# A four-layer graph network on one core: new order of work and a buffer of its own for h ahead of the attention layers

## The chip, the cores and the metric

One core of a Trainium2 chip runs the whole program. The metric is the device time of one execution in microseconds; several runs of a kernel are given by their median. A profile is one such execution, recorded instruction by instruction.

## What is computed

The reference has 3327 nodes with 256 features and a sparse adjacency matrix `adj` (3327 x 3327, int32, about 0.5% ones). Layer 0:

```
h = x @ Wt.T + bt                          # 3327 x 64
s = leaky_relu(h @ Wa.T + ba, 0.2)         # one score per node
scores = where(adj > 0, s, -9e15)
neighbor = softmax(scores, axis=1) @ h
x = layer_norm(x + neighbor @ Wp.T + bp) * gamma + beta
```

The score belongs to the row, so within a row all neighbours have one weight and all others another. Row i of `neighbor` follows from the number of its neighbours, the sum of h over them, and the sum of h over all nodes.

Layers 1 to 3 are attention over the same graph with 8 heads of 32, and a feed-forward part of width 1024:

```
q, k, v = split(layer_norm(x) @ w_qkv)
attn = softmax(where(adj != 0, q @ k.T * 32**-0.5, -inf))
x = x + (attn @ v) @ w_proj + b_proj
x = x + gelu(layer_norm(x) @ w1 + b1) @ w2 + b2
```

## The kernel before, in words

Nodes lie in 26 blocks of 128 rows (`NB`; the last has 127), blocks in 7 groups of four (the last has two). The kernel writes the order of instructions of every engine by hand: each engine runs its instructions in the order in which the Python code issues them, and waits where an operand or a buffer is not ready. So a call's place in the code is its place in five queues at once. TensorE is PE in the profile, VectorE DVE, ScalarE ACT, GpSimd POOL and SyncE SP.

Layer 0 does two things with `adj` at once: it computes the layer, and it makes for each node a list of up to 40 neighbours (`LMAX`), because layers 1 to 3 gather the k and v rows of listed neighbours only. Per block i, `Block` (L694) has these steps:

- `load` (L700): SyncE loads 128 rows of `adj` as int32 into one of three buffers with the tag `a32`.
- `sign` (L707): ScalarE turns them into 0 and 1 in bf16 (`abf`, three buffers); VectorE (blocks 0 to 2) or GpSimd clears the padding column.
- `turn` (L716): TensorE transposes the 26 tiles of 128 x 128, ScalarE copies them to `aT`.
- `candidates` (L726): VectorE multiplies by column numbers (L731) and takes the 8 largest of each of 16 segments of 208 columns (L735).
- `list` (L737): VectorE takes the 40 largest of these 128 (L741 to L748).

For h, `x_turn` (L782) transposes a group of x, `h_of` (L793) multiplies and VectorE adds the bias (L804). `split_h` (L808) writes h as three bf16 parts side by side. `of_h` (L821) makes `S.fold` from the identity, the column sum `S.hsum` (26 fp32 matmuls, L829) and the scores `S.s`. The tile `S.h` (L777) comes from the `a32` buffers. `sums` (L850) multiplies the parts of h by the turned blocks, two blocks at a time.

Per group, `Group` (L841) has the rest of layer 0 as steps: `copy` and `back` (sums out of PSUM and turned back), `soft` (weights; L889 to L918 on VectorE, 12 to 15 small matmuls into `places`, two exponentials on ScalarE, L919), `mix` (L934; it ends by calling `place`, L923, which reads `places` and forms ranks), `project` (L953), `add` (L967, with a norm's statistics), `norm` (ScalarE, L977), `norm1` (L983), `turn1` (L993), `qkv0` and `qkv2` (L1001, two blocks each, with a store of k and v), and `store` (L1018, two stores). `project` and `turn1` and `qkv` share three PSUM banks (`bank`, L628).

The stretch from L1043 to L1079 is written out call by call: three blocks are loaded, signed and turned, the lists of blocks 0 and 1 made, then the groups of h with pieces of blocks 2 and 3 between them, then `split_h`, `sums(1)`, `of_h`, `turn(4)`, `sums(3)`, `copy` of group 0, load, sign and turn of block 5, and `sums(5)`. The loop from L1108 runs over blocks 4 to 25. Each pass loads, signs and turns block i + 2, makes candidates and list of block i, and runs the group steps of two half slots, `plan[2 * i]` ahead of the candidates and `plan[2 * i + 1]` ahead of the list. `plan` (L1083 to L1102) gives each step a half slot:

```
names = ("copy", "back", "soft", "mix", "project", "add", "norm", "norm1", "turn1",
         "qkv0", "qkv2", "store")
...
    at = dict(zip(names, (0, 1, 3, 4, 5, 6, 7, 8, 9, 10, 11, 12)))
    first = 8 * g + 4
    if g == 0:
        first = 8
        at["copy"] = -9
        at["back"] = 0
```

After the loop, nodes are sorted by number of neighbours. The sort's first part (L1128 to L1147) makes ranks, the second (L1153 to L1185) a permutation `perm` by one-hot products (`pp_perm` L1178, `pf` L1182). The last two groups' remaining steps stand around these. GpSimd then gathers the rows of the sorted blocks (`gather_rows`, L1262), loads of weights and biases follow (`load_rest`, L1242), and layers 1 to 3 run over the sorted blocks: GpSimd gathers k and v rows neighbour by neighbour (L1303, 1344 instructions over three layers), VectorE forms scores and weighted values (L1325, L1326, L1366), TensorE adds them up and does the dense parts. All of `Layer` is untouched by the change. A second path for graphs that don't fit (`general_path`) is not taken.

Of the kernel before, what the change touches and what calls it, by code (L numbers as in the profile page):

```python
# [8 lines left out]
FP = mybir.dt.float32  # L9
BF = mybir.dt.bfloat16  # L10
# [7 lines left out]
P = 128  # L18
N = 3327
# [4 lines left out]
H0 = 64  # L24
# [499 lines left out]
def sparse_path(ctx, tc, ins, out, dram, flag):  # L524
# [98 lines left out]
    with tc.tile_pool(name="a", bufs=1) as a, tc.tile_pool(name="aw", bufs=2) as aw, \  # L623
# [42 lines left out]
        nrow = 2 * D + 2 * H0 + 1  # L666
        row = a.tile([1, nrow], FP, name="s_row")
        o = 0
# [5 lines left out]

        zero = a.tile([1, KVW[1]], FP, name="zero")
        nc.vector.memset(zero, 0.0)
# [17 lines left out]
        class Block:  # L694


            def __init__(self, i):
                self.i, self.r = i, ROWS[i]

            def load(self):  # L700
                i, r = self.i, self.r
                a32 = aw.tile([P, N], I32, tag="a32", bufs=3, name=f"s_a32_{i}")
                for p0, p1 in (((0, P),) if r == P else ((0, r // 16 * 16), (r // 16 * 16, r))):
                    nc.sync.dma_start(a32[p0:p1], ins["adj"][i * P + p0:i * P + p1, :])
                self.a32 = a32

            def sign(self):  # L707
                i, r = self.i, self.r
                self.abf = aw.tile([P, PADDED], BF, tag="abf", bufs=3, name=f"s_abf_{i}")

                (nc.vector if i < 3 else nc.gpsimd).memset(self.abf[:, N:], 0.0)  # L711
                if r < P:
                    nc.gpsimd.memset(self.abf[96:P, :], 0.0)
                nc.scalar.sign(self.abf[:r, :N], self.a32[:r])  # L714

# [10 lines left out]
            def candidates(self, part=None):  # L726

                i = self.i
                if not part:
                    v = self.v = aw.tile([P, NSEG, SEG], BF, tag="v", name=f"s_v_{i}")  # L730
                    nc.vector.tensor_mul(v, self.abf.rearrange("p (s c) -> p s c", c=SEG),  # L731
                                         seg1[:, None, :].to_broadcast([P, NSEG, SEG]))
                    self.cand = aw.tile([P, NSEG, 8], FP, tag="cand", name=f"cand_{i}")
                for s in range(NSEG) if part is None else range(part * 4, part * 4 + 4):
                    nc.vector.max(out=self.cand[:, s, :], in_=self.v[:, s, :])  # L735

# [14 lines left out]
        def weights0():  # L751

            S.wtT = a.tile([P, 2, H0], FP, name="s_wtT")

            S.wpT = a.tile([H0 + 1, D], FP, name="s_wpT")
            nc.sync.dma_start(S.wpT[H0:, :], ins["L0_gnn_bp"][None, :])
            S.nT = a.tile([H0 + 1, 512], FP, name="s_nT")
            nc.vector.memset(S.nT[H0:, :], 1.0)
            pt, pt2 = bank("s_pt_w"), bank("s_pt_w2")
            for c in range(2):  # L760
                nc.tensor.transpose(pt[:, c * H0:(c + 1) * H0], wt_raw[:, c * P:(c + 1) * P],
                                    ident[:H0, :H0])
                nc.tensor.transpose(pt2[:H0, c * P:(c + 1) * P], wp_raw[:, c, :], ident)
            nc.scalar.copy(S.wtT, pt[:, :2 * H0].rearrange("p (c h) -> p c h", c=2))
            nc.scalar.copy(S.wpT[:H0], pt2[:H0, :D])
            brow = a.tile([P, nrow], FP, name="s_brow")
            for c0 in range(0, nrow, 512):
                cw = min(512, nrow - c0)
                pb = bank(f"s_pb_row_{c0}")
                nc.tensor.matmul(pb[:, :cw], ones[0:1, :], row[:, c0:c0 + cw],  # L770
                                 start=True, stop=True)
                nc.scalar.copy(brow[:, c0:c0 + cw], pb[:, :cw])
            S.gam_b, S.bet_b = (brow[:, k * D:(k + 1) * D] for k in range(2))
            S.bt_b = brow[:, 2 * D:2 * D + H0]
            S.wa_b = brow[:, 2 * D + H0:2 * D + 2 * H0]
            S.ba_b = brow[:, nrow - 1:nrow]
            S.h = aw.tile([P, NB, H0], FP, tag="a32", bufs=3, name="s_h")  # L777
            nc.vector.memset(S.h[96:P, NB - 1, :], 0.0)
# [41 lines left out]

        def of_h():  # L821

            S.fold = a.tile([P, H0], FP, name="s_fold")
            nc.vector.tensor_copy(S.fold, ident[:, :H0])
            nc.vector.tensor_add(S.fold, S.fold, ident[:, H0:])
            ph = bank("s_phsum")
# [4 lines left out]
            S.hsum = a.tile([P, H0], FP, name="s_hsum")  # L831
            nc.scalar.copy(S.hsum, ph[:, :H0])

            t = aw.tile([P, NB, H0], FP, tag="v", name="s_h_wa")
# [6 lines left out]
        class Group:  # L841
# [92 lines left out]
            def mix(self):  # L934
# [15 lines left out]
                nc.vector.tensor_add(nb, nb, t3)  # L950
                self.place()

# [95 lines left out]
        for i in range(2):  # L1048
# [6 lines left out]
        pieces = [lambda i=i, k=k: blk[i].candidates(k) if k < 4 else blk[i].list()  # L1055
                  for i in (2, 3) for k in range(5)]
        NG = len(GROUPS)
        for g in range(NG):
            x_turn(g)
            if g:  # L1060
                h_of(g - 1)
            if g == 2:
                turn(3)
            if g == 4:
                blk[4].load()
                blk[4].sign()
            for _ in range(2 if g > 3 else 1):
                pieces.pop(0)()
        h_of(NG - 1)
        split_h()  # L1070
        sums(1)
        of_h()
        turn(4)
        sums(3)
        groups[0].copy()
        blk[5].load()
        blk[5].sign()
        turn(5)
        sums(5)  # L1079

        names = ("copy", "back", "soft", "mix", "project", "add", "norm", "norm1", "turn1",  # L1083
                 "qkv0", "qkv2", "store")
        plan = [[] for _ in range(2 * NB)]
        for g in reversed(range(NG)):
            at = dict(zip(names, (0, 1, 3, 4, 5, 6, 7, 8, 9, 10, 11, 12)))
            first = 8 * g + 4
            if g == 0:
                first = 8  # L1090
                at["copy"] = -9
                at["back"] = 0
            elif g == NG - 2:
                at.update(norm=6, norm1=7, turn1=7, qkv0=99, qkv2=99, store=99)
            elif g == NG - 1:
                first = 2 * NB - 4
                at.update(soft=2, mix=3, project=3, add=99, norm=99, norm1=99, turn1=99, qkv0=99,
                          qkv2=99, store=99)
# [9 lines left out]
        for i in range(4, NB):  # L1108
# [3 lines left out]
            for s in plan[2 * i]:  # L1112
                step(*s)
            blk[i].candidates()
            if i + 2 < NB:
# [3 lines left out]
            for s in plan[2 * i + 1]:  # L1119
                step(*s)  # L1120
            blk[i].list()
        last = groups[-2:]
        last[0].qkv(0)
        last[0].qkv(2)
# [23 lines left out]

        last[1].add()
        last[1].norm()  # L1150

# [11 lines left out]
        nc.vector.tensor_copy(num_bf, num)  # L1163
        last[1].norm1()
        last[1].turn1()
        last[1].qkv(0)
        last[1].store()
        oh_lo = aw.tile([P, NB, P], BF, tag="v", name="oh_lo")
# [471 lines left out]
```

## Time and profile before

| What | Value |
|---|---|
| Median of 3 runs | 2555.74 us (2554.16 to 2559.1) |
| Profiled execution, its own time | 2555.05 us |
| Its span, first to last instruction | 2553.3 us |
| Mean granted TensorE clock | 0.782 |
| First gather of sorted rows (L1263, GpSimd) | 498.05 us from the span's start |
| Neighbour gathers, L1303 | 1344 instructions, mean 947 ns, 1272.7 us busy |
| Rows L735, maxima of 8 | 416 instructions, mean 360 ns, 118.0 us busy |
| Row L731, products with column numbers | 26 in layer 0, mean 1883 ns |

A row of the profile names a line of the kernel, an engine, an operation, what is written and read, how many instructions there are and how long they ran. In a timeline a row has its start in the span, its length, and in brackets how long the engine sat idle before it and what ended that. The list of waits sums such idle times by the pair of waiting and releasing lines. The clock is a share of TensorE's full speed. The mean of L735 in the list of groups is that of the records; in a timeline sixteen of them take 4.52 us, since they overlap.

### The profile page before, as it was taken

How to read it: one execution, taken by the hardware profiler on the slowest of the kernel's cores; microseconds unless marked ns; L12 is line 12 of the kernel's file. 1: busy time of each engine (PE TensorE's matmuls, PEld its weight loads, DVE VectorE, ACT ScalarE, POOL GpSimd, SP SyncE). 2: the span in 40 equal slices, each digit the busy share in tenths (PEclk: the TensorE clock that was granted, in tenths of full speed). 3: DMA queues.
4: the chain of work that ended last, by engine and by line, in shares of the span. 5: the costliest groups of instructions: out<-in, count | busy, mean ns of one | idle time of the engine just before them, and what ended most of it. 6: DMA issues, size and time to landing. Idle time of an engine off the chain costs nothing.

```text
span 2553.3 us, 24048 instructions
## 1 busy us (share of the span) xinstructions
PE 1667.7 (65%) x7561; PEld 1119.4 (44%) x7561; DVE 1939.2 (76%) x3983; ACT 781.8 (31%) x1321; POOL 1361.1 (53%) x1458
## 2 busy tenths in 40 slices
PE   5668775426588787865276778777733666766667
PEld 4545553214444454544244445445422444434444
DVE  6697999568888887764788988878537868777864
ACT  5346663201243333332022233333210221222222
POOL 4000000177777776631777767656137767777671
PEclk9768777657788788887577888788865877987888
DMA  6324430377777777753777767756347756766672
GB/s 255 108 98 165 162 116 35 116 232 217 230 211 232 229 220 204 205 117 109 212 210 216 215 190 218 211 174 179 72 152 209 211 169 189 210 187 189 187 193 54
DMA packets 144487, 453.80 MB, mean 178 GB/s; under 512 B 29522, under 2 KB 40157, under 8 KB 141022
## 3 DMA queue, kind: packets, MB, share of 16 engines
q0 software_dynamic: 113056, 370.26, 51.3%
q1 hardware_dynamic: 9834, 53.90, 6.0%
q10 hardware_dynamic: 21458, 28.02, 3.1%
q8 instruction: 61, 1.00, 0.2%
q14 instruction: 78, 0.63, 0.1%
HBM read 420.64 MB, written 31.42 MB: 177 GB/s over the span
## 4 chain that ended last, share of the span: by engine, by line
PE 17%; DVE 15%; DMA 12%; POOL 9%; issue 9%; ACT 2%; DVEq 0%; ACTq 0%; POOLq 0%; SPq 0%
DMA kv<-kv,t 11%; POOL kv L1303 8%; PE pu L1440 5%; PE py L1463 4%; DVE kv L1325 4%; PE po L1372 3%; DVE vw L1366 3%; DVE sc L1326 3%; PE pk L1493 2%; PE po L1396 1%; POOL out_dram L1506 1%; DVE t L1481 1%; DVE st_n L575 1%; PE py L1456 0%; PE pq L1493 0%
## 5 line engine op out<-in xcount | busy, mean ns | idle before, releaser
L1303 POOL DMA_INDIRECT kv<-kv,t x1344 | 1272.7, 947 | 641.3 <-issue 355.7
L1372 PE MATMUL po<-s_ident,vw 128*128 128x128 f32 x2688 | 456.3, 327 | 514.0 <-DVE vw L1366 512.8
L1372 PEld LDWEIGHTS po<-s_ident,vw 128*128 128x128 f32 x2688 | 381.4, 170 | 641.5 <-DVE vw L1366 543.7
L1325 DVE TENSOR_TENSOR kv<-kv,q 128x1024 f32<-128x1024 f32 (+3 forms) x363 | 413.6, 1139 | 311.8 <-DMA kv<-kv,t 195.4
L1326 DVE TENSOR_REDUCE sc<-kv 128x32 f32<-128x1024 f32 (+3 forms) x363 | 414.1, 1141 | 12.4
L1366 DVE TENSOR_TENSOR vw<-kv,w 128x1024 f32<-128x1024 f32 x333 | 372.3, 1128 | 1.7
L1440 PE MATMUL pu<-fT,s_w 128*128 128x512 f32 (+2 forms) x768 | 322.8, 555 | 2.9 <-ACT fT L596 2.9
L1463 PE MATMUL py<-gT,s_w 128*128 128x512 f32 (+1 forms) x672 | 283.6, 550 | 0.0
L1446 ACT ACTIVATE gT<-pu,pvb 128x512 f32<-128x512 f32 (+2 forms) x192 | 116.6, 608 | 380.0 <-PE pu L1440 379.5
L1440 PEld LDWEIGHTS pu<-fT,s_w 128*128 128x128 f32 x768 | 151.8, 211 | 124.8 <-issue 91.1
L711 POOL MEMSET s_abf<- 128x1 bf16 x23 | 2.2, 105 | 356.0 <-DVE s_v L731 239.1
L1463 PEld LDWEIGHTS py<-gT,s_w 128*128 128x128 f32 x672 | 124.6, 192 | 102.9 <-issue 66.1
L735 DVE MAX8 cand<-s_v 128x8 f32<-128x208 bf16 x416 | 118.0, 360 | 0.9
L1493 PE MATMUL pk<-s_w_qkv,nT 128*128 128x512 f32 x208 | 109.6, 653 | 6.1 <-ACT nT L596 6.1
L588 ACT ACTIVATE xn_f<-t,nm_f,rqy_f 128x256 f32<-128x256 f32 x78 | 43.2, 594 | 217.7 <-DVE nm_f L582 211.0
L591 PE MATMUL pf<-s_ident,xn_f 128*128 128x128 f32 x156 | 46.0, 436 | 97.7 <-ACT xn_f L588 97.5
L723 PE MATMUL s_ptb<-s_ident_bf,s_abf 128*128 128x128 bf16 x676 | 67.0, 265 | 64.1 <-ACT s_abf L714 48.7
L1396 PE MATMUL po<-s_w_proj,oT 128*128 128x256 f32 x312 | 101.0, 455 | 0.0
L1340 ACT ACTIVATE sc<-sc,mx 128x120 f32<-128x120 f32 (+6 forms) x78 | 32.0, 410 | 204.9 <-DVE mx L1337 204.4
L723 PEld LDWEIGHTS <-s_abf 128*128 128x128 bf16 x676 | 56.6, 122 | 78.3 <-ACT s_abf L714 55.0
L724 ACT COPY s_aT<-s_ptb 128x896 bf16<-128x896 bf16 x104 | 82.3, 859 | 20.5 <-PE s_ptb L723 20.5
L855 PE MATMUL s_pa<-s_aT,s_hs 128*128 128x256 bf16 x338 | 80.0, 285 | 13.2 <-DVE s_hs L817 13.2
(290 smaller groups left out, 2176.1 us busy)
## 6 DMA issues: line engine op xcount, KB each, us to landing
s_a<-in_adj_dram SPq DMA_DIRECT2D x25, 1663.5 KB
kv<-kv,t POOLq DMA_INDIRECT x1344, 3.8
kv<-kvr ACTq DMA_DIRECT2D x52, 256.0 KB
kv<-s_kvr ACTq DMA_DIRECT2D x26, 256.0 KB
s_w<-in_L_gnn_w_dram SPq DMA_DIRECT2D x6, 1024.0 KB
t<-ql ACTq DMA_DIRECT2D x6, 592.0 KB
t<-s_x ACTq DMA_DIRECT2D x6, 512.0 KB
s_w_qkv<-in_L_gnn_w_qkv_dram SPq DMA_DIRECT2D x3, 768.0 KB
```

Source lines behind the costliest of these rows:

```text
L723: nc.tensor.transpose(pt[:, m, :], self.abf[:, k * P:(k + 1) * P], ident_bf)
L735: nc.vector.max(out=self.cand[:, s, :], in_=self.v[:, s, :])
L1303: nc.gpsimd.indirect_dma_start(out=t[:, s, :], out_offset=None, in_=kv[L], in_offset=bass.IndirectOffsetOnAxis(ap=t2[:, b, k:k + 1].bitcas ...
L1325: nc.vector.tensor_mul(k, k, self.q[b][:, None, :].to_broadcast([P, n, D]))
L1326: nc.vector.tensor_reduce(self.sc[b][:, s0:s0 + n, :], k.rearrange("p s (h d) -> p s h d", d=HD), AX.X, ALU.add)
L1366: nc.vector.tensor_mul(vw[:, :n * D].rearrange("p (s h d) -> p s h d", h=HEADS, d=HD), v, self.wp[b][:, s0:s0 + n, :, None].to_broadcast([ ...
L1372: nc.tensor.matmul(self.po[b][:, k * P:(k + 1) * P], vw[:, at:at + P], ident, is_transpose=True, start=(s0 + s == 0 and k == 0), stop=(s0 ...
L1396: nc.tensor.matmul(ps, c["oT"][:, k * P:(k + 1) * P], w["w_proj"][:, k, :], start=False, stop=(k == 1))
L1440: nc.tensor.matmul(c["pu", f][:, :n], w["w1"][:, e, f * P:(f + 1) * P], c["hT"][:, e, :n], start=(e == 0), stop=(e == 1))
L1446: nc.scalar.activation(g[:, :n], c.pop(("pu", f))[:, :n], AF.Gelu_apprx_tanh, bias=w["b1"][:, f:f + 1])
L1463: nc.tensor.matmul(c["py"][e][:, :n], w["w2"][:, f, e * P:(e + 1) * P], g[:, :n], start=(f == 0), stop=last)
L1493: nc.tensor.matmul(ps[:, :c1 - c0], c["hT"][:, e, j * P:(j + 1) * P], nxt["w_qkv"][:, e, c0:c1], start=(e == 0), stop=(e == 1))
```

## The change

The change is ahead of the layers only; five edits stand in one diff.

- h gets a buffer of its own instead of one of the three `a32` buffers. In return the one-row tiles `row` and `zero` use the buffers with the tag `ql`.
- Block 0 is loaded, signed and multiplied in two column halves (1664 and 1663), each with its own instruction.
- Between the parts of h, the candidates and the list of block 2 come in one piece ahead of h's first part; block 3 follows in five pieces, and a first piece of block 4 is added; its other pieces come after `sums(5)`.
- `S.fold` is made in `weights0`. The column sum (`sum_h`, new, the code is that of `of_h`) comes ahead of `split_h`; load and sign of block 5 come ahead of `sums(1)`; `back` of group 0 ahead of `sums(5)`; `of_h`'s remaining part comes last. The steps of group 0 from `soft` on stand half a slot later, and `place` is a step of its own, next to `project`. Block 4 has nothing to do for VectorE in the loop.
- After the loop, `add` and `norm` of the last group stand ahead of the qkv of the group before, and its `norm1`, `turn1`, `qkv` and `store` ahead of the sort's second part.

```diff
-        row = a.tile([1, nrow], FP, name="s_row")
+        row = aw.tile([1, nrow], FP, tag="ql", name="s_row")
...
-        zero = a.tile([1, KVW[1]], FP, name="zero")
+        zero = aw.tile([1, KVW[1]], FP, tag="ql", name="zero")
...
+                mid = NSEG // 2 * SEG
+                self.cols = [(0, mid), (mid, PADDED)] if i == 0 else [(0, PADDED)]
...
-                    nc.sync.dma_start(a32[p0:p1], ins["adj"][i * P + p0:i * P + p1, :])
+                    for c0, c1 in self.cols:
+                        c1 = min(c1, N)
+                        nc.sync.dma_start(a32[p0:p1, c0:c1],
+                                          ins["adj"][i * P + p0:i * P + p1, c0:c1])
...
-                nc.scalar.sign(self.abf[:r, :N], self.a32[:r])
+                for c0, c1 in self.cols:
+                    c1 = min(c1, N)
+                    nc.scalar.sign(self.abf[:r, c0:c1], self.a32[:r, c0:c1])
...
-                    v = self.v = aw.tile([P, NSEG, SEG], BF, tag="v", name=f"s_v_{i}")
-                    nc.vector.tensor_mul(v, self.abf.rearrange("p (s c) -> p s c", c=SEG),
-                                         seg1[:, None, :].to_broadcast([P, NSEG, SEG]))
+                    self.v = aw.tile([P, NSEG, SEG], BF, tag="v", name=f"s_v_{i}")
...
+                    for c0, c1 in self.cols:
+                        if s * SEG == c0:
+                            nc.vector.tensor_mul(
+                                self.v[:, s:c1 // SEG, :],
+                                self.abf[:, c0:c1].rearrange("p (s c) -> p s c", c=SEG),
+                                seg1[:, None, :].to_broadcast([P, c1 // SEG - s, SEG]))
...
-            S.h = aw.tile([P, NB, H0], FP, tag="a32", bufs=3, name="s_h")
+            S.h = a.tile([P, NB, H0], FP, name="s_h")
...
-                self.place()
...
-                  for i in (2, 3) for k in range(5)]
+                  for i in (2, 3, 4) for k in range(5)]
         NG = len(GROUPS)
         for g in range(NG):
             x_turn(g)
+            if g == 1:
+
+                for _ in range(5):
+                    pieces.pop(0)()
             if g:
                 h_of(g - 1)
+                pieces.pop(0)()
...
-            for _ in range(2 if g > 3 else 1):
-                pieces.pop(0)()
         h_of(NG - 1)
+        sum_h()
         split_h()
+        blk[5].load()
+        blk[5].sign()
         sums(1)
-        of_h()
         turn(4)
         sums(3)
         groups[0].copy()
-        blk[5].load()
-        blk[5].sign()
         turn(5)
+        groups[0].back()
         sums(5)
+        for piece in pieces:
+            piece()
+        of_h()
...
-            at = dict(zip(names, (0, 1, 3, 4, 5, 6, 7, 8, 9, 10, 11, 12)))
+            at = dict(zip(names, (0, 1, 3, 4, 5, 5, 6, 7, 8, 9, 10, 11, 12)))
             first = 8 * g + 4
             if g == 0:
                 first = 8
-                at["copy"] = -9
-                at["back"] = 0
+                at = {k: v + 1 for k, v in at.items()}
+                at["copy"] = at["back"] = -9
...
-            blk[i].candidates()
+            if i > 4:
+                blk[i].candidates()
...
-            blk[i].list()
+            if i > 4:
+                blk[i].list()
         last = groups[-2:]
+        last[1].add()
+        last[1].norm()
         last[0].qkv(0)
...
-        last[1].add()
-        last[1].norm()
+        last[1].norm1()
+        last[1].turn1()
+        last[1].qkv(0)
+        last[1].store()
...
-        last[1].norm1()
-        last[1].turn1()
-        last[1].qkv(0)
-        last[1].store()
```

More of the change, by code (lines that the diff above doesn't have):

```diff
@@ L751, in weights0 @@
         def weights0():
+            S.fold = a.tile([P, H0], FP, name="s_fold")
+            nc.vector.tensor_copy(S.fold, ident[:, :H0])
+            nc.vector.tensor_add(S.fold, S.fold, ident[:, H0:])
             S.wtT = a.tile([P, 2, H0], FP, name="s_wtT")
@@ L819, in split_h, with sum_h @@
             nc.vector.tensor_copy(hs[:, :, 2 * H0:3 * H0], rest)
[L821 to L825, printed above, removed]
+        def sum_h():
             ph = bank("s_phsum")
@@ L832, in of_h @@
             nc.scalar.copy(S.hsum, ph[:, :H0])
+        def of_h():
             t = aw.tile([P, NB, H0], FP, tag="v", name="s_h_wa")
@@ L1075, in sparse_path @@
         groups[0].copy()
-        blk[5].load()
-        blk[5].sign()
         turn(5)
+        groups[0].back()
         sums(5)
-        names = ("copy", "back", "soft", "mix", "project", "add", "norm", "norm1", "turn1",
+        for piece in pieces:
+            piece()
+        of_h()
+        names = ("copy", "back", "soft", "mix", "place", "project", "add", "norm", "norm1", "turn1",
                  "qkv0", "qkv2", "store")
@@ L1096, in sparse_path @@
                 first = 2 * NB - 4
-                at.update(soft=2, mix=3, project=3, add=99, norm=99, norm1=99, turn1=99, qkv0=99,
+                at.update(soft=2, mix=3, place=3, project=3, add=99, norm=99, norm1=99, turn1=99, qkv0=99,
                           qkv2=99, store=99)
```

## The prediction

> **What bounds the kernel now.** I read the page's head first, then busy time by stage over layer 0, then VectorE's waits in layer 0, then the timeline at each of those waits.
>
> ```profile
> span 2553.3 us, 24048 instructions
> PE 1667.7 (65%) x7561; PEld 1119.4 (44%) x7561; DVE 1939.2 (76%) x3983; ACT 781.8 (31%) x1321; POOL 1361.1 (53%) x1458
> ```
>
> The change touches only what lies ahead of the first row gather (GpSimd, 498.05 us). What follows keeps its instructions and hangs on that gather, so a microsecond saved before it is one off the end. By stage (columns: busy PE, PEld, DVE, ACT, POOL, then clock, DMA share and GB/s):
>
> ```profile
> 60.00:125.00 65.00, 39.26 (x348) 35.55 (x348) 43.09 (x127) 22.85 (x24) 0.30 (x3) 0.76 0.32 114
> 260.00:460.00 200.00, 126.52 (x846) 93.43 (x844) 187.70 (x690) 101.24 (x137) 3.88 (x11) 0.75 0.27 93
> ```
>
> From 260 to 460 us VectorE is busy 94% and waits once, 0.79 us: it is the bound, and the change takes no work from it. Ahead of 260 it is not full. Who it waited for until 500 us (total, times, longest):
>
> ```profile
> DVE s_v L731 <- ACT s_abf L714: 20.5, 2, 10.4
> DVE s_h L804 <- PE s_ph L798: 11.8, 4, 4.5
> DVE s_z L938 <- ACT s_m L919: 7.6, 2, 4.4
> DVE s_x L986 <- ACT s_x L980: 7.2, 2, 5.8
> DVE s_x L972 <- PE s_pp L963: 6.8, 3, 5.0
> DVE deg L889 <- ACT s_acc L876: 5.6, 1, 5.6
> DVE place L927 <- PE places L903: 5.3, 2, 2.7
> DVE pf L1182 <- PE pp_perm L1178: 5.2, 1, 5.2
> ```
>
> With 1.5 us at the start these make 71 us, 59.6 of them before block 13's product at 259.13. VectorE's work is fixed, so the gain is the idle time removed. The 10.4 us one, in the timelines of VectorE and ScalarE:
>
> ```profile
> 102.65 1.89 DVE L731 TENSOR_TENSOR s_v<-s_abf,seg 128x3328 bf16<-128x3328 bf16 x1 [10.38 <-ACT s_abf L714]
> ...
> 99.09 0.58 ACT L865 COPY s_sc<-s_pc 65x512 f32<-65x512 f32 x1
> 99.56 2.98 ACT L714 ACTIVATE s_abf<-s_a 128x3327 bf16<-128x3327 int32 x1
> ```
>
> Block 5's sign (99.56) stands in ScalarE's queue behind group 0's copy, which waits for its sums; its load had been issued at 38.24. It is an order, not a transfer. VectorE's times at the two ends of the fixed stretch:
>
> ```profile
> 252.08 0.69 DVE L972 TENSOR_TENSOR s_x<-s_x,s_pp 128x512 f32<-128x512 f32 x1 [5.01 <-PE s_pp L963]
> 477.51 0.69 DVE L986 TENSOR_TENSOR s_x<-s_x,s_brow 128x512 f32<-128x512 f32 x1 [5.85 <-ACT s_x L980]
> 493.58 0.21 DVE L1182 COPY pf<-pp_perm 128x52 f32<-128x52 f32 x1 [5.24 <-PE pp_perm L1178]
> ```
>
> **What the Trainium skill says.** *ScalarE: Activation LUTs*, "What ACT_TABLE_LOAD costs": an activation with immediate scale and bias takes 186 ns + 0.833 ns an element. For 3327 that is 2.96 us; the trace has 2.98. So half a sign is 1.57 us (estimate). *VectorE: DVE Perf Modes*, "The perf-mode tier table": a bf16 product runs two elements a cycle (1224 ns at 2048); the trace's 1.88 us for 3328 lies on that line, half is 1.02 us (estimate). *TensorE: Matmul & The Clock Gate*, "What's actually happening": after about 3.4 us idle the array runs at half clock. The trace agrees: after 13.2 us idle the sums at 77.5 start 0.21 us apart, then 0.11. *DMA: Bandwidth & Descriptors*, "Queues, rings and completion order": descriptors of a ring are consumed in order, so a first half of a load should land near half time. No run here shows it yet.
>
> **The change, part by part.** "Before" and "now" are times from the span's start.
>
> *First block in halves.* The load of block 0 was issued at 3.55 and its sign started at 11.30. From 4.5 to 11.1 us the core moved 2.44 MB; half of that had moved at 8.1. Sign of half one 8.3 to 9.9. Product and eight maxima (8 x 0.28) then run to 13.2, when half two (11.3 to 12.9) is there; done 16.4, before 20.8. List 0 takes 3.75 us: 20.15. ScalarE is 1.3 to 1.4 us earlier only, since block 1's sign follows the turn of all of block 0 (4.3 us): it ends at 20.3. VectorE starts block 1 at 20.4, before 24.5: **4.1 us**, of which 0.15 is paid for the split product. The extra DMA issue is 0.33 us on SyncE, under a queue of loads. Bounds: nothing (halves land together) to 4.4.
>
> *Own buffer for h; `row`, `zero` in other slots.* No engine but the first sign waited for a block's load, so the third load buffer is worth nothing by itself. Loads 3 to 5 go out at 13, 20 and 28 us instead of 22, 29 and 38: 1.7 MB more at some 0.4 MB/us while rows of x are gathered, and GpSimd may end those, then block 3's pad memset, 2 us after 39.97. Block 3's product comes at 42.4 and a wait of 3.7 us follows it, which hides that. 0 to +2; I take 0.
>
> *Lists between the parts of h.* VectorE: block 1 to 30.6, fold and memsets to 31.8, all of block 2 (1.88 + 4.52 + 3.75) to 42.0. h's first part is ready at 41.9 (before 43.2, less 1.3), so the 4.5 goes. The next parts are bound by TensorE, busy from 39.6 to 61.4: 46.0, 51.2, 53.8, 56.4. Between them lie 3.1 us (product, four maxima) and three times 1.2: waits 0, 3.7, 1.1, 1.1, together 5.9 instead of 11.8. List 3, block 4's product and four maxima follow; the split starts at 64.3 (70.46) and ends at 71.3 (77.4): **6.1 us** earlier with 3.5 us more done.
>
> *Column sum ahead of the sums, block 5's sign ahead of the copy.* The 52 passes for hsum took TensorE 5.9 us between two sums; now they run at 64.4 to 70.3 beside VectorE's split, and leave the array warm. If that cover goes, 5.9 comes back. TensorE then: sums 71.3 to 77.1, turn of block 4 to 80, sums to 85.7, turn of block 5 to 89.2 (its sign long done; before, 4.1 us of waiting), back to 90.9, sums to 97, turn 6 to 100. On ScalarE acc ends at 91.4, sign 6 at 94.4, sign 7 at 103.8, turn 7 at 108.2, sign 8 at 111.1; the sums of block 7 end at 113.3. The sign's pad memset on GpSimd moves too: 0.1 us on an idle queue.
>
> VectorE: rest of block 4 from 71.3 to 78.4, `of_h` to 82.6, block 5 with list to 92.8 (no wait, was 10.38), soft to 95.1 (acc at 91.4, was 5.61), block 6's maxima to 101.5.
>
> *Group 0 half a slot later.* A **new wait** is paid here: the exponentials now stand on ScalarE behind group 1's copy, which waits for the sums of block 7. They end at 114.5, so VectorE sits from 101.5 to 114.5: 13.0 us, with mix, list 6 and all else behind it. (Before: 4.38 at 125.24.) Still mix runs 10.7 us earlier, with block 6's 6.4 already done, and the 2.67 for places at 130 is gone. Then without waits: soft of group 1 ends 130.1, add 136.0, list 7 139.8 (before 159.54: 19.7); list 8 160.4 (180.0); add of group 1 166.3; list 9 176.5; norm1 183.8 (1.36 gone); list 10 194.2; list 11 206.7; mix of group 2 there (exponentials 205.6; 3.19 gone); block 12 and place to 216.4 (2.65 gone); list 12 220.2.
>
> TensorE over the same stretch, from the bank that group 1's add frees at 160.9: transposes 163, turn 11 166, sums 172, two pairs of qkv at 5.3 each 182.6, turn 12 185.5, back 189, transposes 193, qkv 201, turn 204, sums 210, qkv 216, sign 14 (ScalarE) 219.8, turn 223.2, projection 226.9 for its first half. So VectorE waits 6.7 and 1.0 at group 2's add, 226.9 for 252.08: **25.2 us** earlier. The other count agrees: idle up to block 13 is 7.2 + 0.3 + 5.9 + 13.0 + 7.7 = 34.1 for 59.6, less 0.15. The moved qkv and store of group 0 take their four ScalarE DMA issues (0.33 to 0.5 us each) past sign 12 and turn 12 in that chain.
>
> *Place apart from mix.* 0.65 us a group, moved behind a block's maxima: counted above at 130 and 236; later it had no wait.
>
> *The stretch to 460* stays 25.2 early.
>
> *Last norms.* Let T be the end of the last list (459.74 before). Add of the last group T to T+4.4, its norm on ScalarE T+4.45 to T+5.5; so group 5's first copy waits 1.3 us, but TensorE needs that bank only at T+7.7. The sort's first part ends at T+9.7, norm1 at T+14.8 (the 5.85 is gone). ScalarE's stores hold it to T+16.6; then transposes, qkv, the permutation at T+26.7 and `pf` at T+27.5, before T+33.84. **6.3 us**. VectorE reaches `pf` at T+22.9 and waits 4.6. The last store moves with it (before 493.85 against `pf` 493.58), so it is no new bound.
>
> Sum: 25.2 + 6.3 = 31.5 us. Against the profiled execution (2555.05: span 2553.3 and 1.75 around it) 2523.5; it lies 0.7 under the median, so **2524**.
>
> **Rivals.**
> *TensorE keeps its pace of before (2534).* It is for this that h's parts are TensorE's. Then the split is 4.8 earlier, hsum gives 5.9 and sign 5 gives 4.1, no more: 14.8 at the copy and at group 2's add, and 6.3 at the end: 21. Against it, the warm start.
> *The second wait closes (2516).* If TensorE's chain from 160.9 to 226.9 ends 7.7 us sooner, VectorE runs through: 39. Against: its transposes and products stand as close as in the trace.
> *The end gives nothing (2530).* If the last stores' landing (493.85, gather 498.05) sets the gather alone and does not move, 25.2 remain. Against it: the stores hang on the same norm.
> *Halves and orders do nothing (2555).* The halves land together, the 13 us wait grows to the 30 it would have to be. The trace has no such stall.
> *Slower (2570).* TensorE holds 17% of the chain that ended last, 434 us, at a mean clock of 0.782. Layer 0 ends sooner and is denser; if the throttle grants less in layers 1 to 3, the whole is slower from a clock of 0.729 (434 x 0.782/0.729 adds 31.5); at 0.707 it adds 46, so 2570. For it: stages differ from 0.5 to 0.91. Against: those layers start alike.
>
> **How the numbers follow.** Forecast 0.56; TensorE's pace 0.18; no end gain 0.10; second wait 0.10; nothing 0.03; slower 0.03. The range goes from the second wait's 2516 to 2538: TensorE's pace (2534) with the halves worth only 2 of their 4.1 us, or with 2 us for the rows of x and the same again elsewhere. It leaves out 0.03 + 0.03 and the outer parts of two cases; the forecast's own bounds (halves 0 to 4.4, rows 0 to +2) lie inside. A run tells apart 0.2%, about 5 us. Faster 0.94, same 0.03, slower 0.03.
>
> **What would show it.** The first product near 9.9 us; no wait at block 5; hsum ending before the first sums; a wait of some 13 us at mix near 114; one of 7 at add near 227; the last list near 434.5, `pf` near 462 and the first row gather near 466.5. I am wrong if VectorE waits anew between 260 and 430, if mix comes after 120, or if layers 1 to 3 take other than 2055 us from the first gather.

## The result and the profile after

| | Before | After |
|---|---|---|
| Median | 2555.69 us (2554.16 to 2559.1) | 2522.66 us (2519.64 to 2524.01, 4 runs) |
| Profiled execution, its own time | 2555.05 us | 2522.87 us |
| First gather of sorted rows | 498.05 us | 468.00 us |
| From that gather to the end of the span | 2055.25 us | 2053.1 us |

The ratio after/before is 0.9867, interval 0.985 to 0.9884. The forecast was 2524. Of the 32.2 us between the two spans, 30.05 lie ahead of the first gather; the other 2.1 are no more than the spread from profile to profile, since the same layers took 2054.6 to 2058.7 in the other profiles of these sessions. In the last session of the study (marked so below) every kernel took some 580 us longer, the one before too (3133.24 us), nearly all of it behind the first gather, so of those runs only ratios and stretches within one profile are used.

The head of the page after (span, then busy time, share and instructions by engine):

```profile
span 2521.1 us, 24055 instructions
PE 1667.8 (66%) x7561; PEld 1121.9 (45%) x7561; DVE 1938.2 (77%) x3984; ACT 781.1 (31%) x1322; POOL 1361.1 (54%) x1458
```

The work is the same (VectorE 1938.2 us after 1939.2). So it is idle time that went. VectorE's waits in the profile after, up to 470 us (total, times, longest):

```profile
DVE s_z L952 <- ACT s_m L933: 13.6, 1, 13.6
DVE s_h L819 <- PE s_ph L813: 10.2, 4, 5.4
DVE s_v L743 <- ACT s_abf L722: 6.5, 2, 6.0
DVE s_x L985 <- PE s_pp L976: 5.8, 4, 4.4
DVE pf L1204 <- PE pp_perm L1200: 4.0, 1, 4.0
DVE s_ident_bf L532 <- POOL s_ident masks.py:199: 1.3, 1, 1.3
```

With 0.4 us of small ones they sum to 41.8 us, where the prediction's list of before comes to 71.8 with all its small ones: 30.0 us less, as at the gather. Read it by names: `s_v` fell from 20.5 to 6.5 (block 5's 10.4 is gone), `deg` (the wait for `acc`, the sums turned back) and `place` are off the list, one of the two `s_z` waits is gone and the other has grown to 13.6. The wait for h has hardly moved. Two stages after, in the columns of the prediction's table:

```profile
60.00:125.00 65.00, 50.55 (x471) 45.83 (x470) 47.97 (x145) 32.30 (x38) 0.30 (x3) 0.89 0.37 132
260.00:460.00 200.00, 134.79 (x810) 96.09 (x809) 185.87 (x676) 95.08 (x136) 3.68 (x9) 0.74 0.29 96
```

In 60 to 125 us VectorE is busy 48.0 us instead of 43.1, so only part of the gain lies there; by group 2's add (252.08 us before, 229.16 after) it has grown to 22.9 us. The second window holds the sort now, too, and stays VectorE's. VectorE's timeline before at the split of h and at mix, and the first gather on GpSimd:

```profile
70.46 1.03 DVE L815 CAST s_hs<-s_h 128x1664 bf16<-128x1664 f32 x1
...
125.24 0.16 DVE L938 TENSOR_TENSOR s_z<-deg,s_m 128x4 f32<-128x4 f32 x1 [4.38 <-ACT s_m L919]
...
498.05 0.98 POOL L1263 DMA_INDIRECT t<-t,perm  x1 [96.95 <-DVE bias L1234]
```

VectorE's timeline after, at the places that the prediction timed, and the first gather again:

```profile
10.21 1.02 DVE L743 TENSOR_TENSOR s_v<-s_abf,seg 128x1664 bf16<-128x1664 bf16 x1 [6.00 <-ACT s_abf L722]
...
20.64 1.91 DVE L743 TENSOR_TENSOR s_v<-s_abf,seg 128x3328 bf16<-128x3328 bf16 x1
...
68.56 1.03 DVE L830 CAST s_hs<-s_h 128x1664 bf16<-128x1664 f32 x1
...
100.10 1.89 DVE L743 TENSOR_TENSOR s_v<-s_abf,seg 128x3328 bf16<-128x3328 bf16 x1 [0.53 <-ACT s_abf L722]
120.13 0.16 DVE L952 TENSOR_TENSOR s_z<-deg,s_m 128x4 f32<-128x4 f32 x1 [13.58 <-ACT s_m L933]
...
229.16 0.69 DVE L985 TENSOR_TENSOR s_x<-s_x,s_pp 128x512 f32<-128x512 f32 x1 [4.36 <-PE s_pp L976]
...
445.79 0.68 DVE L999 TENSOR_TENSOR s_x<-s_x,s_brow 128x512 f32<-128x512 f32 x1
462.94 0.21 DVE L1204 COPY pf<-pp_perm 128x52 f32<-128x52 f32 x1 [3.97 <-PE pp_perm L1200]
...
468.00 0.97 POOL L1285 DMA_INDIRECT t<-t,perm  x1 [90.32 <-DMA colsb<-in_L_gnn_be_dram]
```

The line at 100.10 is block 6's product: at block 5's nothing is waited for. The line at 445.79 is the last group's norm, where 5.85 us used to stand and no bracket stands now.

### The profile page after: what moved, and what is told of

Read it like the earlier page. It is cut to its first block, busy times and chain, and to the rows that moved or that the text cites. A ratio compares the mean times of both kernels' runs of the same rounds, so it can differ in the third digit from the quotient of the medians.

```text
span 2521.1 us, 24055 instructions
## 1 busy us (share of the span) xinstructions
PE 1667.8 (66%) x7561; PEld 1121.9 (45%) x7561; DVE 1938.2 (77%) x3984; ACT 781.1 (31%) x1322; POOL 1361.1 (54%) x1458
## 3 DMA queue, kind: packets, MB, share of 16 engines
q0 software_dynamic: 113056, 370.26, 51.6%
## 4 chain that ended last, share of the span: by engine, by line
PE 19%; DVE 14%; DMA 12%; POOL 9%; issue 8%; ACT 2%; DVEq 0%; POOLq 0%; ACTq 0%
DMA kv<-kv,t 12%; POOL kv L1325 8%; PE pu L1462 6%; PE py L1485 5%; PE po L1394 4%; DVE kv L1347 4%; DVE vw L1388 3%; DVE sc L1348 2%; PE pk L1515 2%; PE po L1418 1%; POOL out_dram L1528 1%; DVE st_n L575 1%; DVE t L1503 1%; PE pq L1515 0%; PE py L1478 0%
## 5 line engine op out<-in xcount | busy, mean ns | idle before, releaser
L1412 ACT COPY oT<-po 128x256 f32<-128x256 f32 x78 | 28.8, 370 | 198.3 <-PE po L1394 197.7
```

## The experiments

"Split" is the start of the first cast of h (68.56 above), "mix" the first line on `s_z` (120.13), "add" that of group 2 (229.16), "gather" the first gather of sorted rows. Each mark is read in one profile of the kernel, since the marks tell apart what the medians don't; each ratio is to the kernel before in the same session.

| Kernel | Split | Mix | Add | Gather | Split to gather | Median, ratio to before |
|---|---|---|---|---|---|---|
| before | 70.46 | 125.24 | 252.1 | 498.05 | 427.6 | 2555.69 |
| after | 68.56 | 120.13 | 229.2 | 468.00 | 399.4 | 2522.66, 0.9867 (0.985 to 0.9884) |
| e1 block 0 whole | 70.37 | 121.85 | 230.9 | 469.11 | 398.7 | 2525.3, 0.9869 (0.985 to 0.9889) |
| e2 h in a load buffer | 65.80 | 117.73 | 226.8 | 465.71 | 399.9 | 2523.5, 0.9858 (0.984 to 0.9876) |
| e3 last norms late | 68.80 | 120.59 | 229.7 | 474.64 | 405.8 | 2530.39, 0.9886 (0.9868 to 0.9904) |
| e4 hsum behind the sums | 68.19 | 125.53 | 234.7 | 473.75 | 405.6 | 2532.29, 0.9892 (0.9873 to 0.991) |
| own buffer only, on before | 72.81 | 127.53 | 254.4 | 500.33 | 427.5 | 2558.41, 0.9995 (0.9986 to 1.0005) |
| e6 exponentials first | 68.45 | 116.69 | 225.5 | 465.43 | 397.0 | 2524.06, 0.9855 (0.9829 to 0.9881) |
| e7 e6, mix behind list 6 | 68.96 | 116.79 | 225.2 | 465.10 | 396.1 | 2519.74, 0.9843 (0.9821 to 0.9866) |
| e8 e7, h in a load buffer | 64.48 | 111.97 | 220.0 | 459.92 | 395.4 | 2516.58, 0.9836 (0.9812 to 0.986) |
| *last session:* e5 sign 5 late | 78.38 | 136.50 | 245.2 | 484.15 | 405.8 | 3108.23, 0.9923 (0.9897 to 0.9949) |
| last norms only, on before | 74.50 | 130.62 | 257.9 | 497.29 | 422.8 | 3125.78, 0.9984 (0.9971 to 0.9998) |
| e9 two load buffers | 84.35 | 136.79 | 245.9 | 484.39 | 400.0 | 3104.6, 0.9904 (0.9879 to 0.993) |
| e10 e7, two load buffers | 72.38 | 120.02 | 228.2 | 467.57 | 395.2 | 3092.55, 0.9878 (0.9856 to 0.99) |

My theory: four parts of the change each take a named wait from VectorE, the halves, the place of hsum, the place of block 5's sign and the last norms, and h's own buffer gives nothing. The chief rival: TensorE's chain sets the stretch whatever VectorE does, so that single parts are swallowed.

**e1, the halves undone.**

```diff
-                self.cols = [(0, mid), (mid, PADDED)] if i == 0 else [(0, PADDED)]
+                self.cols = [(0, mid), (mid, PADDED)] if i < 0 else [(0, PADDED)]
```

> The changed kernel with block 0 loaded, signed and multiplied whole again. Theory (TensorE's line through the parts of h, the sums and the turns sets the end): block 0's sign ends 1.3 to 1.4 us later, VectorE's 4.1 us are swallowed by its waits for the parts of h, and the first row gather comes 1 to 2 us later than 468.0: 2524. Rival (VectorE's own line sets the end): the first product 4 us later and all of it kept, gather at 472, 2527.

The gather moved by 1.1 us. VectorE's first product came 3.9 us later (14.12), and about half of it was given back before the split, which is 1.8 us later; mix and group 2's add are 1.7 later. VectorE's timeline of e1 at h's parts shows how:

```profile
56.40 0.42 DVE L819 TENSOR_TENSOR s_h<-s_ph,s_brow 128x256 f32<-128x256 f32 x1 [5.31 <-PE s_ph L813]
```

VectorE still waits 5.3 us here for TensorE, against 5.41 at the same place after, and the wait of 1.72 ahead of it is gone. The halves make VectorE early for a meeting whose time TensorE sets. What they do bring comes by ScalarE: block 1's sign starts at 16.49 us after and at 18.39 in e1, so that TensorE's line is 1.9 us earlier.

**e2, h in one of the three load buffers again.**

```diff
-            S.h = a.tile([P, NB, H0], FP, name="s_h")
+            S.h = aw.tile([P, NB, H0], FP, tag="a32", bufs=3, name="s_h")
```

> The changed kernel with h back in one of the three load buffers. Theory: no engine waits for a load of adj, so nothing: first gather at 468 +- 1, 2523 +- 2. Rival (the third load buffer is the gain): loads of blocks 5 to 7 late, a sign waits, 5 us or more: 2528 and up.

The own buffer gives nothing. It even goes with a later split, by 2.8 us (65.80 against 68.56), and a gather 2.3 us later; the medians can't tell that apart.

**The own buffer alone, on the kernel before** (its three lines of the diff).

> The kernel before with h in its own buffer and the two one-row tiles in the other slots, nothing else. Theory A (the early loads of adj slow TensorE in the parts of h; with h in a load buffer the changed kernel began its split at 65.8, with its own at 68.2 to 68.8): the split 2 to 3 us later than 70.5, and a gather 1 to 3 us later than 498.0. Theory B (a chance of the clock in one execution): split at 70.5 +- 0.5 and gather at 498 +- 0.5. Rival of the prediction (the buffer is a gain): gather at 490 or less.

No gain: ratio 0.9995. Split and gather came 2.35 and 2.3 us later, the same sign and size as between e2 and after.

**e3, the last norms back in their old place.**

```diff
         last = groups[-2:]
-        last[1].add()
-        last[1].norm()
...
-        last[1].norm1()
-        last[1].turn1()
-        last[1].qkv(0)
-        last[1].store()
+        last[1].add()
+        last[1].norm()
...
         nc.vector.tensor_copy(num_bf, num)
+        last[1].norm1()
+        last[1].turn1()
+        last[1].qkv(0)
+        last[1].store()
```

> The changed kernel with the last group's add, norm, norm1, turn and qkv where they stood before. Theory: VectorE waits some 5.9 us for the last norm again and some 5 for the permutation, first gather 6 to 7 us later, 474 to 475, 2529. Rival (the last stores' landing alone sets the gather): same, 2523.

Split to gather grew by 6.4 us, and both waits of before are back in VectorE's timeline of this kernel:

```profile
454.20 0.69 DVE L999 TENSOR_TENSOR s_x<-s_x,s_brow 128x512 f32<-128x512 f32 x1 [5.56 <-ACT s_x L993]
...
470.13 0.21 DVE L1204 COPY pf<-pp_perm 128x52 f32<-128x52 f32 x1 [5.10 <-PE pp_perm L1200]
```

The rival that the end gives nothing falls.

**The last norms alone, on the kernel before** (last session).

> The kernel before, with only the last group's add and norm ahead of the qkv of the group before, and its norm1, turn1, qkv and store ahead of the sort's second part. Theory (this part gives the same on either kernel, since the stretch before it is VectorE's): the wait of 5.85 at the norm is gone, first gather 6.3 to 6.7 us earlier, at 491.5, median 2549. Rival: it only pays together with the rest, first gather within 2 us of 498.

The stretch from group 2's add to the gather, which doesn't hold the early waits, fell from 245.97 to 239.40 us, by 6.6. The norm at 475.25 has no wait. The ratio agrees (0.9984; 0.16% of 3133 is 5 us, with 0.6 to 9 in the interval). So this part adds up, whichever kernel it is put on.

**e4, hsum between the sums again.**

```diff
         h_of(NG - 1)
-        sum_h()
         split_h()
...
         sums(1)
+        sum_h()
         turn(4)
```

> The changed kernel with the column sum of h behind the first sums, as before the change. Theory: TensorE's line gets 5.9 us longer ahead of group 0's mix, VectorE's wait there grows from 13.6 to 19, and 5 to 6 us remain at group 2's add and at the end: gather at 473 to 474, 2528. Rival (TensorE has room: its first sums run colder without the column sum ahead, or a later wait of VectorE has slack): 2 us or less.

Every mark behind the split is 5.4 to 5.8 us later. Here the place was not what I expected: the wait at mix did not grow to 19, it stayed near that (13.93), and the loss stands as a wait for `acc` ahead of it, in VectorE's timeline of e4:

```profile
102.20 0.17 DVE L903 COPY deg<-s_acc 128x4 f32<-128x4 f32 x1 [5.41 <-ACT s_acc L890]
...
125.53 0.16 DVE L952 TENSOR_TENSOR s_z<-deg,s_m 128x4 f32<-128x4 f32 x1 [13.93 <-ACT s_m L933]
```

In the kernel after VectorE doesn't wait for `acc`. Here it is held there for 5.4 us, and the exponentials at the other end come 5.4 us later too, so the stretch keeps its length and is shifted as a whole.

**e5, load and sign of block 5 behind group 0's copy** (last session).

```diff
         split_h()
-        blk[5].load()
-        blk[5].sign()
         sums(1)
...
         groups[0].copy()
+        blk[5].load()
+        blk[5].sign()
         turn(5)
```

> The kernel after, with load and sign of block 5 back behind group 0's copy. Theory: the transposes of block 5 wait for a sign of 3 us that stands behind a copy which waits for its sums, so everything of TensorE behind them is some 4 us later: mix near 124, first gather near 472. Rival: VectorE's idle time at mix takes it all, or ScalarE has room: first gather 468 as before this edit.

From split to mix it took 58.1 us, against 51.6 after, and from split to gather 405.8 against 399.4: 6.3 us, more than the 4 that I took for the transposes' wait. The old wait is back, at block 5's product, in VectorE's timeline of e5:

```profile
105.14 1.90 DVE L743 TENSOR_TENSOR s_v<-s_abf,seg 128x3328 bf16<-128x3328 bf16 x1 [8.37 <-ACT s_abf L722]
...
136.50 0.16 DVE L952 TENSOR_TENSOR s_z<-deg,s_m 128x4 f32<-128x4 f32 x1 [12.38 <-ACT s_m L933]
```

Against e9 of the same session (the kernel after with two load buffers) it is 5.7; kernels of one edit order agree in this stretch across sessions within 1 us (e9 and after 400.0 and 399.4, e10 and e7 395.2 and 396.1).

**e6, the exponentials ahead of group 1's copy.** ScalarE's timeline after, ahead of mix:

```profile
118.93 0.58 ACT L878 COPY s_sa<-s_pa 128x512 f32<-128x512 f32 x1 [2.82 <-PE s_pa L869]
119.41 0.58 ACT L879 COPY s_sc<-s_pc 65x512 f32<-65x512 f32 x1
119.89 0.21 ACT L933 ACTIVATE s_m<-s_m 128x4 f32<-128x4 f32 x1
```

The exponentials (119.89) stand behind a copy that waits for the sums. The edit turns that half slot round:

```diff
                     plan[k].append((g, name))
+        plan[12].reverse()
```

> The changed kernel with group 0's exponentials ahead of group 1's copy on ScalarE. Theory (the new wait at mix is that copy's place in the queue, and what VectorE gains there reaches the end): mix at 116.5 instead of 120.1, gather 3.6 us earlier, 464.4, 2519. Rival (TensorE's line takes it back at group 2's add, where VectorE waited 4.4 us): wait there grows to 8, gather at 468, 2523.

VectorE's timeline of e6 at mix:

```profile
116.69 0.16 DVE L952 TENSOR_TENSOR s_z<-deg,s_m 128x4 f32<-128x4 f32 x1 [9.68 <-ACT s_m L933]
```

Mix came 3.4 us earlier, as expected, and group 2's add 3.7; at the gather 2.6 were left. So 3.9 of the 13.6 us were the order of these three lines, and in e6 the exponentials (116.45) follow directly on what ScalarE has ahead of them, the turned copies of block 7 and the sign of block 8 (113.57).

**e7, mix of group 0 behind list 6 as well.**

```diff
                 at = {k: v + 1 for k, v in at.items()}
+                at["mix"] = 6
                 at["copy"] = at["back"] = -9
```

> As the run with the exponentials ahead, and group 0's mix behind list 6 instead of ahead of it, so that VectorE makes the list (3.75 us) while it would wait. Theory: wait at mix 6 instead of 13.6, gather 7.3 us earlier than 468.0, 460.7, 2515. Rival (TensorE's line takes it back): 464 to 468.

The wait fell to 5.83, and new ones took its place, in VectorE's timeline of e7:

```profile
116.79 0.16 DVE L952 TENSOR_TENSOR s_z<-deg,s_m 128x4 f32<-128x4 f32 x1 [5.83 <-ACT s_m L933]
...
130.34 0.69 DVE L985 TENSOR_TENSOR s_x<-s_x,s_pp 128x512 f32<-128x512 f32 x1 [1.11 <-PE s_pp L976]
132.05 0.69 DVE L985 TENSOR_TENSOR s_x<-s_x,s_pp 128x512 f32<-128x512 f32 x1 [1.02 <-PE s_pp L976]
```

The gather is 0.3 us earlier than e6's: the rival holds for this part, TensorE's line swallows it.

**e8, e7 with h in a load buffer** (e2's edit).

> As the run before, and h in one of the load buffers again. Theory A (early loads slow TensorE in the parts of h): split at 65.8, gather 2 to 2.5 us earlier than in the run before, 458.4, 2513. Theory B (chance): no difference beyond 0.5 us.

Gather at 459.92, 5.2 us earlier than e7 and more than twice what I expected, and 8.1 earlier than after. At 2516.58 us it is the fastest kernel of the study; its interval (0.9812 to 0.986) still overlaps that of after.

**e9 and e10, two load buffers** (last session). They were to tell what about h's buffer delays the split: the earlier loads (theory A: with three buffers free the loads go out at 13, 20 and 27 us and the DMA engines are full until 45), or h's place (theory B).

```diff
-                a32 = aw.tile([P, N], I32, tag="a32", bufs=3, name=f"s_a32_{i}")
+                a32 = aw.tile([P, N], I32, tag="a32", bufs=2, name=f"s_a32_{i}")
```

> The kernel after, with two buffers for block loads in place of three; h keeps its own buffer. The load of block 2 waits for the first block's sign, and each later load stands one block later in the queue. Theory A (the early loads, which fill the DMA engines until 45 us, go with TensorE's slow stretch): split at 65.5 to 66.5 us in place of 68.56, slow stretch over by 46 to 51 us, DMA share in 40 to 45 us well below 0.99, first gather 465.5 to 466.5. Theory B (it is h's place in memory, not the loads): split at 68.5, first gather 468. If block 2's data come too late for its sign, its product would wait on VectorE and the split would come later than 68.5.

> The kernel after with the exponentials ahead of the copy, group 0's mix behind list 6, and two load buffers with h in its own. Theory A: like the same edits with h in a load buffer: split 64.5, mix 112, first gather 460, median 2516 to 2518. Theory B: like those edits with three buffers: split 69, mix 116.8, gather 465, median 2520 to 2524.

These two don't settle it. Both are the same program up to the split, and it came at 84.35 in one and 72.38 in the other. In that session TensorE and ScalarE stood still ahead of 40 us, for up to 5 us at a time, and in many of these gaps the trace names no instruction that was waited for. But they show two things. The first: e9 and e10 are one program here, and in e10 the 14 transposes at 52.11 took 0.94 us, in e9 those at 63.41 took 1.70. So TensorE's slow pace isn't set by the program alone. For the second, TensorE's lines at 61.70 and 63.41 in e9, and the engines' table from 60 to 65 (columns as above):

```profile
61.70 1.91 PE L813 MATMUL s_ph<-s_wtT,s_xT 128*128 128x64 f32 x8
63.41 1.70 PE L731 MATMUL s_ptb<-s_ident_bf,s_abf 128*128 128x128 bf16 x14
```

```profile
60.00:65.00 5.00, 5.00 (x31) 4.95 (x31) 3.25 (x10) 1.19 (x2) 0.00 (x0) 1.00 0.00 0
```

The 14 transposes took 1.70 us, as in after, where before and e8 have 0.94 for the same 14; and the DMA share was 0.00. So full DMA engines at the moment aren't what makes TensorE slow, which takes the ground from theory A in its plain form.

**What was not undone alone.** Of the theory's four parts the place of hsum, block 5's sign and the last norms hold; for the halves it is mostly the rival that holds. At the gather the single parts give 1.1 us (halves), 5.75 (place of hsum), 5.7 to 6.3 (block 5's sign) and 6.4 to 6.6 (last norms): about 20 of the 30 us. No run undoes the order of the lists between the parts of h, or group 0's later slot with `place` apart. That the other 10 us are theirs is read from the lists of waits; no run shows it.

## Why the prediction was right, step by step

The sum was right: 31.5 us forecast ahead of the gather, 30.05 measured. That it came so close is partly luck. Three of its terms promised too much, and a fourth, TensorE's chain up to group 2's add, was counted too long and made up for most of that.

*First block in halves: the prices right, the worth not.* Half a sign took 1.59 us (estimate 1.57), half a product 1.02 (1.02). The half signs started at 8.59 and 11.52 us (8.3 and 11.3), so the halves of the load were usable one after the other, which agrees with the Trainium skill, where descriptors of one ring are consumed in order (*DMA: Bandwidth & Descriptors*, "Queues, rings and completion order"). The first product came at 10.21 (9.9), block 1's at 20.64 (20.4). But of the 4.1 us, e1 finds 1.7 at group 2's add and 1.1 at the gather.

*Lists between the parts of h: the term that failed.* "The next parts are bound by TensorE" was right, its pace was not. I took its pace of before. TensorE's timelines, before and then after, for the same eight transposes of x and around them:

```profile
49.74 1.04 PE L788 MATMUL s_px<-s_ident,s_x 128*128 128x128 f32 x8
```

```profile
50.64 1.91 PE L803 MATMUL s_px<-s_ident,s_x 128*128 128x128 f32 x8
```

Before, TensorE came up to full pace at about 46 us; after, at about 53. In between, the h part took 3.68 us for 2.61, block 3's first 14 transposes 1.70 for 0.94, the transposes of x 1.91 for 1.04: 2.7 us in three groups. (The last of the three was worth nothing alone: in e6 these transposes took 1.05 us, TensorE then waited 0.82 us for ScalarE, and the split came at 68.45.) VectorE's waits there came to 10.2 us, not 5.9, and the split to 68.56, not 64.3. The gain of 6.1 was 1.9. What the term missed shows in e8, where full pace came at about 45 us and the wait shown further below is absent too. The forecast has the parts of h at 41.9, 46.0, 51.2, 53.8 and 56.4 us and the split at 64.3. VectorE's timeline of e8, whose other edits lie behind the split:

```profile
42.33 0.42 DVE L819 TENSOR_TENSOR s_h<-s_ph,s_brow 128x256 f32<-128x256 f32 x1
46.20 0.42 DVE L819 TENSOR_TENSOR s_h<-s_ph,s_brow 128x256 f32<-128x256 f32 x1 [0.41 <-PE s_ph L813]
51.45 0.42 DVE L819 TENSOR_TENSOR s_h<-s_ph,s_brow 128x256 f32<-128x256 f32 x1 [3.71 <-PE s_ph L813]
54.06 0.42 DVE L819 TENSOR_TENSOR s_h<-s_ph,s_brow 128x256 f32<-128x256 f32 x1 [1.08 <-PE s_ph L813]
56.68 0.42 DVE L819 TENSOR_TENSOR s_h<-s_ph,s_brow 128x256 f32<-128x256 f32 x1 [1.07 <-PE s_ph L813]
...
64.48 1.03 DVE L830 CAST s_hs<-s_h 128x1664 bf16<-128x1664 f32 x1
```

Not all of the delay is pace, though. In TensorE's timeline after, the transposes ahead of a later part of h stand in two fours with a wait for ScalarE's copy between them, where e2 (the second cut below) and e8 have eight in a row:

```profile
54.39 0.61 PE L803 MATMUL s_px<-s_ident,s_x 128*128 128x128 f32 x4
55.73 0.66 PE L803 MATMUL s_px<-s_ident,s_x 128*128 128x128 f32 x4 [0.73 <-ACT s_xT L805]
```

```profile
52.58 1.04 PE L803 MATMUL s_px<-s_ident,s_x 128*128 128x128 f32 x8
```

From the first transpose to the next product of h this is 1.83 us after and 0.88 in e2. All kernels with both the new order and h's own buffer have this wait; why it goes with the buffer is open.

*Column sum beside the split: the place right, the warm start not.* hsum ran from 64.15 to 70.12 beside VectorE's split, and e4 prices the place at 5.4 to 5.8 us (5.9). "And leave the array warm" was wrong, as TensorE's lines after show:

```profile
72.64 0.28 PE L869 MATMUL s_pa<-s_aT,s_hs 128*128 128x256 bf16 x1 [2.52 <-DVE s_hs L832]
75.63 0.43 PE L871 MATMUL s_pc<-s_aT,s_hs 128*65 128x256 bf16 x1 [2.71 <-DVE s_hs L834]
...
79.91 0.34 PE L871 MATMUL s_pc<-s_aT,s_hs 128*65 128x256 bf16 x1
80.08 0.27 PE L869 MATMUL s_pa<-s_aT,s_hs 128*128 128x256 bf16 x1
```

The first product, on the finished part of h, runs at once and the others wait for VectorE's last cast. Across the two gaps TensorE is busy for 0.28 us of 5.5; then it starts 0.21 us apart, and is at 0.11 only from 80 us. The sums took 7.9 us, not 5.8. This agrees with the Trainium skill (*TensorE: Matmul & The Clock Gate*, "What's actually happening": after some 3.4 us idle the clock is halved) only if one short product doesn't count as activity.

*Block 5's sign and the sums: right.* No wait at block 5, none for `acc`; e5 brings the first back and costs 6.3 us.

*The new wait at mix: mechanism and size right, time late.* 13.0 us forecast, 13.58 measured. It came at 120.13 instead of 114.5, by the 4.3 of the split and the 2.1 of the cold sums, less 0.8. "If mix comes after 120" was named as a sign of being wrong, and it came. So did another, a new wait of VectorE between 260 and 430 us, though small: 0.24 us at 288.95 and 1.02 at 290.65, both at group 3's add. e6 confirms what mix waits for.

*Where the 5.6 us went.* Two stages on, at group 2's add, only 2.3 were left: 229.16 for 226.9. It was not slack that took them up. From mix to that add it is 109.0 to 109.2 us in after and in e1 to e4, although mix lies anywhere between 117.7 and 125.5: what mix is late, the add is late too. But the forecast has 112.4 us for this stretch (114.5 to 226.9). TensorE's chain there was counted some 3 us too long: from 160.9 to 226.9 it has 66.0 us, and after, from the end of group 1's first addition at 166.2 to the add at 229.16, it took 63.0. For instance, `back` of group 2 took 2.0 us (191.67 to 193.63) where the forecast has 3.5. So VectorE waited 4.36 + 0.17 us at the add, where I had 6.7 + 1.0. Two errors nearly cancelled. Block 13's product came at 235.36 (233.9), a gain of 23.8 for 25.2.

*Last norms: right.* 6.3 forecast; e3 and the kernel with this part alone give 6.4 to 6.6. `pf` at 462.94 (462) waits 3.97 us (4.6).

*Rivals.* "TensorE keeps its pace" (2534) was nearest to what happened in h's parts and still missed: the split was only 1.9 us earlier, less than its 4.8, but the gain from mix to group 2's add, from 5.1 us to 22.9, came all the same. The end gives its share (e3). Layers 1 to 3 took 2053.1 us from the gather, so the throttle's rival did not come.

## What to carry to other kernels

Value an early start at the next place where the two engines meet: 4 us gained on VectorE were worth 1 to 2, since TensorE set that meeting. Before a delay is put down as taken up by slack, compare the distance to the next mark over several kernels: here what mix was late reached group 2's add in full, and the total came out near because another term was wrong the other way. A duration from the profile of before holds only if the engine's pace does; where a stretch of matrix products follows on half pace, take half pace for all of it as the other bound. Ask of each queue what waits at its head: hsum and block 5's sign paid because each was moved ahead of an instruction that was waiting anyway.

## What the hardware showed that I had not expected

- TensorE's half pace lasted longer than a short warm-up, and not equally long. By the durations of like instructions, and with no pause over 1.1 us in between, it held from 26.81 until about 53 us after (26 us), from 26.70 until about 45 in e8 (18 us), from 42.83 until about 66 in e9 (23 us), and in e10, the same program as e9 up to the split, from 40.35 until about 46 (6 us). The Trainium skill (*TensorE: Matmul & The Clock Gate*, "What's actually happening") has some 3.4 us of steady work until full pace; the shortest stretches here, in e10 and in the last norms alone, are 5 to 6 us. What held the pace down is open.
- It doesn't go with h's buffer. In e2, with h in a load buffer, TensorE held half pace until about 50.5 us as well, as the same 14 transposes show:

```profile
46.27 1.70 PE L731 MATMUL s_ptb<-s_ident_bf,s_abf 128*128 128x128 bf16 x14
```

What does go with the buffer is a later split: 68.2 to 69.0 us in all five kernels with halves outside the last session (after, e3, e4, e6, e7), and 65.8 and 64.5 without it. The wait between the two fours gives 1 us of that; for the rest, e2 came to the same four transposes of x 1.3 us earlier (36.59 for 37.92), and e8 came to full pace sooner. With one profile per kernel, chance is not ruled out for these.
- The granted clock in the table of stages reads 1.00 from 50 to 55 us after, where the eight transposes took 1.91 us, and 1.00 for the same stage before, where they took 1.04. The durations tell the pace; in the profile after that column did not. In the profile before it did: it reads 0.50 from 40 to 45 us and 0.89 from 45 to 50.
- Moving block loads some 9 us earlier (block 3's from 21.61 to 13.14) did not delay the gathers of x: block 3's pad memset on GpSimd came at 40.20 us, before at 39.97.
